# Groups of two batches with 256-column q/k products in place of groups of four with 512

## The chip, the cores and the metric

One core of one Trainium2 chip. The metric is the device time of one execution in microseconds (us).

## The reference, cut to what matters

Four graph layers over 128 batches of 128 nodes x 512 features, all in float32, each followed by a residual and a layer norm. The change touches only the last one, a masked multi-head attention:

```python
# layer 3, x: (128 batches, 128 nodes, 512), 8 heads of 64
qkv  = x @ w_qkv
attn = softmax(where(adj == 0, -inf, q @ k.T * 64**-0.5))
o    = (attn @ v) @ w_proj + b_proj
out  = o + layernorm(o) * gamma + beta
```

## The kernel before

Python chains (one per batch, some per group) ask a small planner, `Plan`, for their turn on an engine and for buffers. The planner holds its own estimate of every duration and fixes one static order of all instructions. So a change of group size or of a buffer count changes two things: the instructions of q and k, and the order of everything.

```python
G = 4                                   # batches that share one xT and the q/k products
BUFS = {"tr": 3, "mm": 3, "sc": 1, ..., "xT": 1, "v": 8, "qkT": 2, ...}

class Plan:
    def at(self, r):                    # earliest start of a request, by the planner's clock
        engine, _, take, _, _ = r["want"]
        t = max(r["ready"] + (MARGIN if engine == "PE" else 0.0), self.free.get(engine, 0.0))
        return max([t, *(self.slots[name][self.next[name]] for name in take())])
    def run(self):                      # the earliest request next; ties: urgent, then rank
        while self.requests:
            t, _, _, n = min((self.at(r), r["want"][4], r["rank"], n)
                             for n, r in enumerate(self.requests))
            ...                         # cut

def query_key(gr, c):                   # one of 8 chains of a group: 128 rows of q or k
    yield gr.turned                     # all G batches are turned into xT
    yield w3_in
    ...                                 # cut: ask for PE, a PSUM bank, and once for qkT
    p = product(lambda k: wqkv_sb[:, k, c * P : (c + 1) * P], lambda k: gr.xT[:, k, :])
    gr.read("xT", G + 2 * K)            # xT is free after the group's q, k and v products
    ...                                 # cut: copy to qkT, ACT for q, DVE for k

# per batch: mixed (L203) -> product (L195) -> ... -> turn into xT (L534) -> values ->
#   scores (L553, 64-row tiles) -> softmax -> two DMAs turn the probabilities ->
#   probabilities times v (L600, 64-column tiles) -> projection (L195) -> norm -> store
```

The last four batches are started 16 ranks early.

## Time and profile before

| | |
|---|---|
| time | 3414.68 us, median of 3 (3414.14 to 3414.78) |
| TensorE busy | 3378.9 of 3412.8 us |
| records of 512 columns for q and k | 2048 |
| TensorE waits shown | 24 us in 3412.8 |

The lines of the page for the q/k products and for the two copies out of PSUM. The columns are: line, engine, operation, output and inputs, shapes, count, then busy us, mean ns of one record, then idle time of the engine before them with what ended it. PE is TensorE, PEld its weight loads, DVE VectorE, ACT ScalarE and POOL GpSimd.

```profile
L195 PE MATMUL mm<-xT,wqkv_sb 128*128 128x512 f32 x2048 | 898.7, 594 | 5.2 <-DVE x L481 2.9 <-DVE qkT L442 1.5 <-ACT xT L536 0.8
L442 DVE COPY qkT<-mm 128x512 f32<-128x512 f32 x128 | 87.3, 682 | 247.4 <-PE mm L195 247.2
L440 ACT ACTIVATE qkT<-mm 128x512 f32<-128x512 f32 x128 | 75.4, 589 | 383.0 <-PE mm L195 383.0
```

The mean of 594 ns is the length of one record from start to end. Records overlap, so the cost of one is the distance between two starts, 429 ns. The copies have 247 and 383 us of idle time ahead of them: they wait for TensorE, never the reverse for long.

The end of the run, from TensorE's timeline (start, length, group, idle before it with what ended it):

```profile
3359.63 1.16 PE L553 MATMUL sc<-qkT 64*128 64x128 f32 x16
...
3373.80 1.16 PE L553 MATMUL sc<-qkT 64*128 64x128 f32 x16
3378.09 1.98 PE L600 MATMUL tr<-prT,v 128*64 128x128 f32 x16 [3.13 <-DMA prT<-p_d]
3381.73 5.17 PE L195 MATMUL mm<-wproj_sb,oT 128*128 128x512 f32 x8 [1.67 <-ACT oT L609]
...
3399.54 3.70 PE L195 MATMUL mm<-wproj_sb,oT 128*128 128x512 f32 x8 [0.74 <-ACT oT L609]
```

After its last scores TensorE has nothing to do until the first probabilities arrive (3.13 us). The wait costs twice: the next two chains take 1.98 and 5.17 us where the same chains take 1.09 and 3.70 elsewhere. The busy time by stretch shows a granted clock of 0.76 from 3380 to 3390 us.

### The profile page before, as it was taken

The page shows a single profiled execution, that of the slowest core. Times are in us where ns is not written, and L with a number is a line of the kernel's source. Part 1 is how long each engine was busy: PE and PEld are TensorE (multiplying, and loading weights), DVE is VectorE, ACT ScalarE, POOL GpSimd, SP SyncE. Part 2 cuts the span into 40 slices and gives each one's busy share as a digit, 9 for nine tenths or more (in the row PEclk, how much of TensorE's full clock was granted, in tenths as well). Part 3 has the DMA queues.
Part 4 walks back from the last instruction along what each step waited for, and adds up shares of the span by engine and source line. Part 5 has one row for each costly group of instructions (what it writes and reads, how often), then busy time and mean ns, then how long its engine had stood idle before and what let it go on. Part 6 is the DMA issues. An engine that isn't in the chain of part 4 may idle for free.

```text
span 3412.8 us, 39442 instructions
## 1 busy us (share of the span) xinstructions
PE 3378.9 (99%) x13193; PEld 1727.3 (51%) x13193; DVE 2588.1 (76%) x5399; ACT 1251.9 (37%) x3585; POOL 981.2 (29%) x1031
## 2 busy tenths in 40 slices
PE   9999999999999999999999999999999999999998
PEld 5555555545455455455555555555555545555543
DVE  7776976788777787777877777877778777797766
ACT  3433343334334233342343333433324334244332
POOL 2222422223221333223332223322233222341222
PEclk9999999999999999999999999999999999999999
DMA  4022121202121122111222112221112211121112
GB/s 155 32 86 71 54 75 56 87 30 78 67 77 53 47 78 78 62 60 46 79 76 68 62 48 71 78 68 65 56 56 78 77 60 59 50 78 59 53 69 79
DMA packets 169354, 228.58 MB, mean 67 GB/s; under 512 B 43456, under 2 KB 117312, under 8 KB 169152
## 3 DMA queue, kind: packets, MB, share of 16 engines
q1 hardware_dynamic: 169152, 226.08, 19.5%
q8 instruction: 104, 1.70, 0.2%
q14 instruction: 98, 0.80, 0.1%
HBM read 116.98 MB, written 109.05 MB: 66 GB/s over the span
## 4 chain that ended last, share of the span: by engine, by line
PE 92%; DVE 7%; issue 1%; DMA 0%; ACT 0%; POOL 0%; SPq 0%; POOLq 0%; DVEq 0%; ACTq 0%
PE mm L195 73%; PE tr L203 6%; PE sc L553 4%; PE tr L600 4%; PE mm L515 3%; PE tr L534 2%; DVE st L161 1%; DVE scr L488 1%; DVE x L182 0%; DVE x L507 0%; DVE mv L163 0%; DVE x L481 0%; PE tr L380 0%; DVE x L506 0%; DVE ve L165 0%
## 5 line engine op out<-in xcount | busy, mean ns | idle before, releaser
L195 PE MATMUL mm<-w_sb,yT 128*128 128x512 f32 x2048 | 921.0, 595 | 0.5 <-ACT yT L206 0.5
L195 PE MATMUL mm<-xT,wqkv_sb 128*128 128x512 f32 x2048 | 898.7, 594 | 5.2 <-DVE x L481 2.9
L168 POOL TENSOR_TENSOR rstd<-ve,neghalf 128x1 f32<-128x1 f32 x640 | 446.4, 698 | 1268.5 <-DVE ve L165 1103.3
L195 PEld LDWEIGHTS mm<-xT,wqkv_sb 128*128 128x128 f32 x2048 | 384.7, 190 | 468.5 <-issue 447.0
L195 PEld LDWEIGHTS mm<-w_sb,yT 128*128 128x128 f32 x2048 | 375.5, 190 | 410.4 <-issue 398.1
L195 PE MATMUL mm<-wqkv_sb,xT 128*128 128x512 f32 x1024 | 467.2, 599 | 0.0
L195 PE MATMUL mm<-wproj_sb,oT 128*128 128x512 f32 x1024 | 458.1, 596 | 3.8 <-ACT oT L609 3.8
L188 POOL TENSOR_TENSOR x<-x,beta_sb 128x512 f32<-128x512 f32 x128 | 186.0, 1463 | 937.4 <-PE tr L534 937.4
L571 ACT ACTIVATE pr<-pr,nmx 128x128 f32<-128x128 f32 x1024 | 398.8, 394 | 137.3 <-DVE nmx L567 137.2
L161 DVE BATCH_NORM_STATS2 st<-x 128x6 f32<-128x512 f32 x512 | 349.9, 683 | 4.7 <-ACT x L522 3.4
L177 ACT ACTIVATE x<-x,nmr,rstd 128x512 f32<-128x512 f32 x256 | 206.0, 810 | 288.1 <-DVE nmr L175 284.2
L195 PEld LDWEIGHTS mm<-wproj_sb,oT 128*128 128x128 f32 x1024 | 191.8, 191 | 234.5 <-issue 227.6
L560 DVE TENSOR_TENSOR pr<-sc,maskb 128x1024 f32<-128x1024 f32 x128 | 156.6, 1224 | 191.0 <-PE sc L553 185.3
L195 PEld LDWEIGHTS mm<-wqkv_sb,xT 128*128 128x128 f32 x1024 | 187.0, 190 | 208.7 <-issue 200.6
L442 DVE COPY qkT<-mm 128x512 f32<-128x512 f32 x128 | 87.3, 682 | 247.4 <-PE mm L195 247.2
L206 ACT COPY yT<-tr 128x512 f32<-128x512 f32 x256 | 148.3, 584 | 292.6 <-PE tr L203 290.8
L188 POOL TENSOR_TENSOR x<-x,o 128x512 f32<-128x512 f32 x128 | 180.2, 1408 | 153.6 <-DVE o L617 153.1
L440 ACT ACTIVATE qkT<-mm 128x512 f32<-128x512 f32 x128 | 75.4, 589 | 383.0 <-PE mm L195 383.0
L488 DVE SCALAR_TENSOR_TENSOR scr<-x,wa_rows 128x512 f32<-128x512 f32 x256 | 200.5, 783 | 9.4 <-ACT x L177 3.0
L188 POOL TENSOR_TENSOR x<-x,bias_sb 128x512 f32<-128x512 f32 x128 | 176.7, 1387 | 67.8 <-PE tr L203 57.1
L571 ACT ACTIVATION_READ_ACCUMULATOR pr<-pr,nmx 128x1 f32 x1024 | 195.3, 191 | 0.0
L609 ACT COPY oT<-tr 128x512 f32<-128x512 f32 x128 | 75.0, 586 | 273.4 <-PE tr L600 273.2
(65 smaller groups left out, 3753.6 us busy)
## 6 DMA issues: line engine op xcount, KB each, us to landing
p_d<-pt SPq DMA_DIRECT2D x128, 512.0 KB, 2.6
prT<-p_d SPq DMA_DIRECT2D x128, 512.0 KB, 3.7
x<-in_x SPq DMA_DIRECT2D x128, 256.0 KB, 2.6
out<-x SPq DMA_DIRECT2D x128, 256.0 KB, 2.0
e_d<-et SPq DMA_DIRECT2D x64, 128.0 KB, 1.7
eT<-e_d SPq DMA_DIRECT2D x64, 128.0 KB, 2.2
wqkv_sb<-in_L_gnn_w_qkv SPq DMA_DIRECT2D x1, 3072.0 KB, 10.8
w_sb<-in_L_gnn_weight SPq DMA_DIRECT2D x1, 1024.0 KB, 5.7
```

The source lines that it names most:

```text
L161: nc.vector.bn_stats(st, src)
L168: nc.gpsimd.tensor_tensor(rstd, ve, neghalf, op=ALU.pow)
L177: nc.scalar.activation(xb, xb, AF.Identity, bias=nmr, scale=rstd)
L188: nc.gpsimd.tensor_tensor(dst, dst, other, op=ALU.add)
L195: nc.tensor.matmul(p, lhs(k), rhs(k), start=(k == 0), stop=(k == K - 1))
L203: nc.tensor.matmul(p[:, k, :], xb[:, k * P : (k + 1) * P], nodes, start=True, stop=True)
L206: nc.scalar.copy(yT, p)
L488: nc.vector.scalar_tensor_tensor(scr, xb, 1.0, wa_rows[:, j, :], op0=ALU.mult, op1=ALU.mult, accum_out=gr.s[:, b, j : j + 1],)
L553: nc.tensor.matmul(sc[:, j, c, :], gr.qkT[rws, c, nodes], gr.qkT[rws, K + c, nodes], start=True, stop=True,)
L560: nc.vector.tensor_tensor(pr, sc.rearrange("p j c m -> p (j c) m"), maskb[:, None, :].to_broadcast([P, H, P]), op=ALU.add,)
L571: nc.scalar.activation(pr[:, j, :], pr[:, j, :], AF.Exp, bias=nmx[:, j : j + 1], accum_out=sums[:, j : j + 1],)
L600: nc.tensor.matmul(p[j * HD : (j + 1) * HD, c, :], valued.v[:, (2 * c + j) * HD : (2 * c + j + 1) * HD], prT[:, j * K + c], start=True, st ...
```

## The change

The intent: smaller groups let q, k and the scores of a pair start without waiting for four batches, and more buffers let the next pair be turned while the last is still read. The PSUM tile of a product stays 512 columns wide, so that two blocks of q or k rows of a pair (2 x 256) share one tile and one copy.

```diff
-G = 4
+G = 2
-    ... "xT": 1, "v": 8, "qkT": 2,
+    ... "xT": 2, "v": 8, "qkT": 3,
-            self.turned, self.qk = Event(G), Event(2 * K)
+            self.turned, self.qk = Event(G), Event(K)
-            for n in range(2 * K):
-                plan.start(query_key(groups[g], n // 2 + K * (n % 2)), g * G + n / (2 * K) - ...)
+            for n in range(K):
+                plan.start(query_key(groups[g], n // 2 * 2 + K * (n % 2)), g * G + n / K - ...)
@@ query_key
-        p = product(lambda k: wqkv_sb[:, k, c * P : (c + 1) * P], lambda k: gr.xT[:, k, :])
-        gr.read("xT", G + 2 * K)
+        p = bank([P, 2, G * P], "mm")
+        for j in range(2):
+            for k in range(K):
+                nc.tensor.matmul(
+                    p[:, j, :], wqkv_sb[:, k, (c + j) * P : (c + j + 1) * P], gr.xT[:, k, :],
+                    start=(k == 0), stop=(k == K - 1),
+                )
+        gr.read("xT", G + K)
# cut: the copies write qkT[:, c : c + 2, :]; the load order is kept as it was for groups of four
```

More of the change, by code (lines that the diff above doesn't have):

```diff
@@ L30 @@
     "tr": 3, "mm": 3, "sc": 1,
-    "x": 16, "yT": 3, "e": 2, "et": 1, "eT": 2, "ex": 2, "xT": 1, "v": 8, "qkT": 2,
+    "x": 16, "yT": 3, "e": 2, "et": 1, "eT": 2, "ex": 2, "xT": 2, "v": 8, "qkT": 3,
     "pr": 2, "pt": 1, "prT": 2, "oT": 2, "o": 2,
@@ L273, in loads @@
         landing(bias0_in, P)
-        for i in range(2, G):
+        for i in range(2, 4):
             yield from load(i)
@@ L281, in loads @@
         plan.start(logit_rows(a_sb, slot), 0)
-        for i in range(G, 2 * G):
+        for i in range(4, 8):
             yield from load(i)
@@ L289, in loads @@
         landing(scalars_in, 2 * P)
-        for i in range(2 * G, 3 * G):
+        for i in range(8, 12):
             yield from load(i)
@@ L297, in loads @@
         landing(w3_in, (4 * K + 3) * P)
-        for i in range(3 * G, NB):
+        for i in range(12, NB):
             yield from load(i)
@@ L367, in group @@
                 plan.start(attention1(groups[g], h), g * G + 2 * h - (16 if g * G >= NB - 4 else 0))
-            for n in range(2 * K):
-                plan.start(query_key(groups[g], n // 2 + K * (n % 2)), g * G + n / (2 * K) - (16 if g * G >= NB - 4 else 0))
+            for n in range(K):
+                plan.start(query_key(groups[g], n // 2 * 2 + K * (n % 2)), g * G + n / K - (16 if g * G >= NB - 4 else 0))
         return groups[g]
@@ L435, in query_key @@
             bp = got
-        p = product(lambda k: wqkv_sb[:, k, c * P : (c + 1) * P], lambda k: gr.xT[:, k, :])
-        gr.read("xT", G + 2 * K)
+        p = bank([P, 2, G * P], "mm")
[6 more added lines that the diff above has]
+        gr.read("xT", G + K)
         yield use("ACT" if c < K else "DVE", 0.69, urgent=True)
+        dst = gr.qkT[:, c : c + 2, :]
         if c < K:
-            nc.scalar.mul(gr.qkT[:, c, :], p, HD**-0.5)
+            nc.scalar.mul(dst, p, HD**-0.5)
         else:
             nc.vector.tensor_copy(
-                gr.qkT[:, c, :].rearrange("p (b c r) -> p b c r", b=G, c=Q),
-                p.rearrange("p (b r c) -> p b c r", b=G, c=Q),
+                dst.rearrange("p j (b c r) -> p (j b) c r", b=G, c=Q),
+                p.rearrange("p j (b r c) -> p (j b) c r", b=G, c=Q),
             )
@@ L459, in values @@
         give(bp)
-        gr.read("xT", G + 2 * K)
+        gr.read("xT", G + K)
         event.slot = bv
```

## The prediction

> **What bounds the kernel now.** I read the page first (busy shares, slices, chain that ended last), then the TensorE instruction groups with their shapes, then the timeline of TensorE in the middle and at both ends, then TensorE's waits, then busy time per stretch.
>
> From the page:
>
> ```profile
> PE 3378.9 (99%) x13193; PEld 1727.3 (51%) x13193; DVE 2588.1 (76%) x5399; ACT 1251.9 (37%) x3585; POOL 981.2 (29%) x1031
> PEclk9999999999999999999999999999999999999999
> PE 92%; DVE 7%; issue 1%; DMA 0%; ACT 0%; POOL 0%; SPq 0%; POOLq 0%; DVEq 0%; ACTq 0%
> ```
>
> TensorE is busy for 3378.9 of 3412.8 us, at full granted clock, and is 92% of the chain that ended last. Only 33.9 us is idle. But a busy PE need not be at its peak, so I need the time from one matmul start to the next. The timeline of TensorE, middle of the run (start, length, instructions), gives it:
>
> ```profile
> 2002.18 13.90 PE L195 MATMUL mm<-xT,wqkv_sb 128*128 128x512 f32 x32
> 2015.91 0.38 PE L380 MATMUL tr<-ident,s 128*128 128x128 f32 x2
> ...
> 2031.05 3.70 PE L195 MATMUL mm<-wqkv_sb,xT 128*128 128x512 f32 x8
> 2034.68 1.16 PE L553 MATMUL sc<-qkT 64*128 64x128 f32 x16
> 2035.77 3.70 PE L195 MATMUL mm<-wqkv_sb,xT 128*128 128x512 f32 x8
> ...
> 2095.43 2.84 PE L203 MATMUL tr<-adjT,x 128*128 128x128 f32 x24
> ```
>
> Each float32 product shows as two MATMUL records (a 4-step chain is x8); a transpose as one. Thirty-two records of 512 columns start at 2002.18 and what follows starts at 2015.91: 13.73/32 = **429 ns** each, across four chain ends with no gap. Twenty-four of 128 columns take 2098.10 - 2095.43 = 2.67 (the next record starts at 2098.10): **111.3 ns** each. Two numbers thus fix the cost of a record by its width.
>
> Does that account for the whole? Records of 512 columns: 2048 + 2048 + 1024 + 1024 + 256 = 6400, times 0.429 = 2746 us. Full-array records of 128 columns: 2697 x 0.1113 = 300 us. A score chain (x16) takes 1.09 us to the next start, and the 8-record chain after it 3.63 where 8 x 0.429 is 3.43, so 1.29 x 128 = 165 us. The chains on prT and v take about 1.03 plus two losses of 0.1 around them: 1.23 x 128 = 157 us. Sum 3368, against 3379 busy. So the kernel is a sum of matmuls at their steady pitch, plus mode changes; the bound is **the amount of TensorE work**, not its waits.
>
> The waits of TensorE, whole run (us in total, times, longest), show what a better order could still win:
>
> ```profile
> PE mm L195 <- ACT oT L609: 3.8, 4, 1.7
> PE tr L600 <- DMA prT<-p_d: 3.1, 1, 3.1
> PE mm L195 <- DVE x L481: 2.9, 1, 2.9
> PE tr L203 <- DMA x<-in_x: 2.8, 2, 1.5
> PE tr L305 <- DMA adj_sb<-in_adj: 2.8, 1, 2.8
> PE mm L515 <- DVE qkT L442: 2.7, 1, 2.7
> PE mm L195 <- DVE qkT L442: 1.5, 1, 1.5
> ```
>
> By stretch: about 7.7 us idle in the first 60 us (start-up loads; PE is busy 14.41, 18.76 and 19.13 of three times 20 us), 8.5 us between 400 and 1600 us (397.58 of 400 and 793.85 of 800), nothing from 1600 to 3300, and in the last 53 us 16.9 + 7.7 + 8.5 + 3.2 = 36.3 busy, so some 16.6 us idle. Of these about 9.5 us follow the last product (it starts at 3399.54 and ends at 3403.24): the last batch's normalisation and store.
>
> **What the Trainium skill says.** "TensorE: Matmul & The Clock Gate", section "Back-to-back issue gap", gives N/2.4 ns + 2.5 ns for a warm, isolated matmul. A float32 record here seems to take two array cycles a column: 512 x 2/2.4 + 2.5 = 429.2, and the trace's 429 agrees. For 128 it gives 109.2, the trace has 111.3, so the fixed part is 2.5 to 5 ns. The same page, section "Step-by-step: what each phase is for", says that the next weights load while this matmul runs; the trace agrees, as loads of 190 ns (mean) vanish under a 429 ns pitch and even under 111 ns (eight loads in 0.97 us). "TensorEngine Tiling (Array Packing)", section "Key Properties", says that changing tiling mode drains TensorE; the 0.1 to 0.2 us lost beside each 64-row or 64-column chain agrees. "PSUM — Partial Sum Buffer", section "The four PSUM rules", forbids two open accumulation groups in one bank; the new code closes the first half's before it opens the second's, so it is legal and needs no wait.
>
> **The change, part by part.**
>
> 1. **Twice as many q/k records, half as wide.** Before: 32 groups x 8 chains x 8 records = 2048 of 512 columns. After: 64 groups x 4 double chains x 2 x 8 = 4096 of 256. Columns in all are unchanged, the weights for q and k are loaded twice as often. Pitch at 256: a straight line through 111.3 (128) and 429 (512) gives 111.3 + 128 x 317.7/384 = 217.2 ns; the skill's form gives 256 x 2/2.4 + 2.5 = 215.8. Two of them cost 434.4 or 431.6 in place of 429: +2.6 to +5.4 ns for each of the 2048 old records, **+5 to +11 us**, all on the path, because TensorE is the bound. I take +8.
> 2. **Weight loads.** 2048 more, at 190 ns and pulled ahead. At a pitch of about 216 they stay covered: the 128-column chains already sustain one every 111 ns. Cost 0.
> 3. **Accumulation.** The same 256 columns are added to again after 216 ns. The `mixed` chains accumulate two records on the same 128 columns at 111 ns pitch with no loss. Cost 0.
> 4. **Copies out of PSUM.** 64 x 4 = 256 copies of 512 columns, as before 32 x 8: ACT 589 ns and DVE 682 ns each. The innermost runs (32) and element counts stay. Cost 0, and hidden anyway: DVE has 24% spare, ACT 63%.
> 5. **Buffers.** xT goes from one buffer of four batches to two of two: equal bytes, but the next pair may be turned while the previous one is still read. qkT goes from two of four to three of two: 24 KB a partition in place of 32. This removes waits only where TensorE waits, and that is nowhere from 1600 to 3300 us. The 7.1 us under L481 and L442 are mid-run and could go or move: I take -3.
> 6. **Tail.** Before, the last group computes all eight q/k chains (64 records, 27 us) and only then its scores; DVE is busy only 7.53 of 20 us there, from 3340 to 3360. The last scores end near 3374.9 and the program 38 us later, with about 19 us of products left. After, the first pair's softmax runs beside the second pair's q/k products; the last pair then has one round of softmax and transfers (first score end to first use: 3360.7 to 3378.1, 17.4 us), less product work to fill it (some 9 us plus leftovers of the first pair), and the same 15 us from its last prT chain to the end. I estimate T + 33 in place of T + 38, with T up to a few us later: between -7 and +5, I take -3.
> 7. **Start.** Unchanged: bound by loads and by the adjacency, before any q/k chain (the first starts at 108 us).
>
> Sum: 3414.7 + 8 - 3 - 3, about **3417 us**.
>
> **The rivals.**
>
> (a) *A narrower matmul costs more than the line says*, for instance because a 190 ns load no longer hides under a 216 ns record when chains switch. If the pitch were 232, 4096 x 15 = +61 us, near 3478. For: the loads come almost back to back. Against: the 111 ns pitch with the same loads.
>
> (b) *The order gets worse.* The static plan is recomputed with other ranks and granularity; a pair of batches gives TensorE less independent work ahead, and DVE (76% overall, 38 of 40 us in 60 to 100) could become the local bound. For: q/k now arrive every 27 us in 14 us blocks, and each waits for only two turns. Against: 16 batches are in flight and other chains fill gaps; no wait on PE in the second half. Worth +5 to +40 us.
>
> (c) *The order gets better.* Bubbles (8.5 us) and the avoidable tail (about 7 us) go entirely: 3414.7 + 8 - 15, near 3407. The gain cannot be larger: 33.9 us is all the idle time there is, and some 17 us of that is loads and the last batch's own chain.
>
> (d) *Mode changes move.* Their count stays at 128 score and 128 prT chains, but which neighbour they have may change; at 0.1 us each, up to 10 us either way.
>
> **Range and chances.** The sure part is +5 to +11 us; tail and bubbles span about -15 to +15 around it, and (b) stretches the upper side. I choose 3403 to 3437. A gain of 2% is 68 us, twice the whole idle time: 0.01. A loss of 68 us needs (a) or a bad (b): 0.02. Within 2%: 0.97.
>
> **What would show each step right or wrong.** In the profile after: 4096 records `mm<-xT,wqkv_sb` of 128x256; in the timeline 64 of them from start to next start in 13.8 to 13.9 us (step 1); if it is 14.5 or more, (a) holds. Their mean length should be 592 - 256/1.2, about 379 ns. TensorE busy should rise to about 3384 to 3390 and its waits stay under 40 us; waits on DVE of tens of us mean (b). The 400 to 1600 stretch shows step 5, the last 53 us step 6. Copies at 589 and 682 ns confirm step 4. I am wrong if the pitch is off the line, or if the new order idles TensorE.

## The result

The changed kernel takes **3410.36 us** (median of 4, 3409.27 to 3411.25) against 3414.73 us before (median of 4, 3414.14 to 3417.1). The ratio is 0.9986, 95% interval 0.9968 to 1.0003. The ranges don't overlap, but the interval just touches 1: within 2%, and 4.4 us shorter by the medians.

From the page of the changed kernel, the busy line and the groups that answer to those of before:

```profile
PE 3379.5 (99%) x15241; PEld 2119.6 (62%) x15241; DVE 2593.1 (76%) x5399; ACT 1264.8 (37%) x3585; POOL 947.0 (28%) x1031
L439 PE MATMUL mm<-xT,wqkv_sb 128*128 128x256 f32 x4096 | 911.8, 380 | 0.0
L449 DVE COPY qkT<-mm 128x512 f32<-128x512 f32 x128 | 87.9, 687 | 150.5 <-PE mm L439 149.8
L447 ACT ACTIVATE qkT<-mm 128x512 f32<-128x512 f32 x128 | 76.3, 596 | 278.3 <-PE mm L439 278.0
```

There are twice the records, 380 ns long (379 was expected), and the same copies. TensorE is busy 3379.5 us, 0.6 more than before, though the narrower records alone should add 5. So something else on TensorE got shorter. Its timeline in the middle of the run:

```profile
2010.40 10.52 PE L439 MATMUL mm<-xT,wqkv_sb 128*128 128x256 f32 x48
2020.76 0.60 PE L541 MATMUL tr<-ident,x 128*128 128x128 f32 x4
...
2053.16 1.09 PE L607 MATMUL tr<-prT,v 128*64 128x128 f32 x16
2054.19 1.16 PE L560 MATMUL sc<-qkT 64*128 64x128 f32 x16
2055.28 3.70 PE L195 MATMUL mm<-w_sb,yT 128*128 128x512 f32 x8
```

The first two lines give the pitch: (2020.76 - 2010.40)/48 = 215.8 ns. The last three show what is new in the order: a probabilities chain and a score chain, both on 64-wide tiles, stand **next to each other**. Counted over the whole program, that happens at 28 places; in the kernel before at one.

The waits of TensorE (us in total, times, longest) and the end of its timeline:

```profile
PE tr L380 <- DVE scr L495: 6.4, 6, 2.0
PE tr L607 <- DMA prT<-p_d: 4.1, 3, 3.1
...
PE mm L195 <- ACT oT L616: 1.5, 2, 0.7
```

```profile
3369.60 1.16 PE L560 MATMUL sc<-qkT 64*128 64x128 f32 x16
3370.69 3.70 PE L195 MATMUL mm<-wqkv_sb,xT 128*128 128x512 f32 x8
...
3385.55 1.30 PE L607 MATMUL tr<-prT,v 128*64 128x128 f32 x16 [3.08 <-DMA prT<-p_d]
3387.59 6.44 PE L195 MATMUL mm<-wproj_sb,oT 128*128 128x512 f32 x8 [0.73 <-ACT oT L616]
3394.47 1.09 PE L607 MATMUL tr<-prT,v 128*64 128x128 f32 x16 [0.45 <-DMA prT<-p_d]
3396.31 3.70 PE L195 MATMUL mm<-wproj_sb,oT 128*128 128x512 f32 x8 [0.74 <-ACT oT L616]
```

The waits on the q/k copies are gone, others on DVE came. After the last scores three batches are left to finish in place of four, and after the wait for prT two in place of four. The wait of 3 us and the slow chain after it (6.44 us) are still there. "TensorE: Matmul & The Clock Gate" of the Trainium skill, section "HAM oscillation — how this bites in real kernels", warns of idle gaps of TensorE above some 3.4 us. In these traces shorter gaps were followed by a lower clock: after those of 3.08 and 3.13 us the granted clock was 0.50 for some 6.8 us. Two gaps in the middle (2.05 us, ending at 2862.8, in the changed kernel; 2.91 us, ending at 1260.5, before) were followed by 0.50 for some 3.4 us, while two others (2.05 us at 1437.8; 2.68 us at 857.4) were not. The account below counts what these stretches cost as loss, about 4.4 us before and 4.9 in the changed kernel.

**An account of TensorE.** For every record I took the time to the next record's start and split it: steady pitch (429.05 ns for 512 columns, 215.8 for 256, 111.3 for 128, and half of that, as a convention, for a 64-wide record), idle time that the profile shows, and the rest, which I call loss. The first 2.7 us, before TensorE's first record, are left out. The three add up to the start of the last record; then some 10 us follow.

| us | steady pitch | loss | idle | sum |
|---|---|---|---|---|
| before | 3273.6 | 104.9 | 21.4 | 3399.9 |
| changed | 3278.8 | 100.3 | 17.6 | 3396.7 |
| difference | +5.2 | -4.6 | -3.8 | -3.2 |

And the loss sits at a few kinds of places, each of them almost constant. Between 60 and 3300 us of the kernel before, the means are: 93 ns at the last full-width record ahead of a 64-wide chain; 146 to 147 ns at the end of a 64-wide chain; 91 to 102 ns in the first records after it. A score or a probabilities chain alone thus costs about 0.34 us besides its own work. Where two of different kind stand together, one entry (93) and one aftermath (104, the median) fall away, **0.197 us**. Where two probabilities chains stand together, a lone one's 147 ns end shrinks to 47 as well and the second runs 51 ns shorter, about 0.35 us (the last two from the run e14 below). For the change: 27 more places x 0.197 = 5.3 us, and the loss fell by 4.6.

So the theory is: the narrow records cost 5 us, the new order saves about as much at mode changes of TensorE (from full-width to 64-wide chains and back), and waits fall by 4 us, most of it at the end.

### The profile page after: what moved, and what is told of

Same layout as the page of the kernel before. It is cut to its first block, busy times and chain, and to the rows that moved or that the text cites. A ratio compares the mean times of both kernels' runs of the same rounds, so it can differ in the third digit from the quotient of the medians.

```text
span 3409.4 us, 43497 instructions
## 1 busy us (share of the span) xinstructions
PE 3379.5 (99%) x15241; PEld 2119.6 (62%) x15241; DVE 2593.1 (76%) x5399; ACT 1264.8 (37%) x3585; POOL 947.0 (28%) x1031
## 4 chain that ended last, share of the span: by engine, by line
PE 89%; DVE 9%; DMA 1%; issue 1%; ACT 0%; POOL 0%; SPq 0%; POOLq 0%; DVEq 0%; ACTq 0%
PE mm L195 46%; PE mm L439 25%; PE tr L203 5%; PE sc L560 4%; PE tr L607 4%; PE mm L522 3%; DVE st L161 2%; PE tr L541 2%; DVE scr L495 1%; DVE x L182 1%; DVE x L488 1%; DVE x L636 1%; DVE mv L163 0%; DVE t L633 0%; DVE ve L165 0%
## 5 line engine op out<-in xcount | busy, mean ns | idle before, releaser
L439 PE MATMUL mm<-xT,wqkv_sb 128*128 128x256 f32 x4096 | 911.8, 380 | 0.0
L439 PEld LDWEIGHTS mm<-xT,wqkv_sb 128*128 128x128 f32 x4096 | 771.1, 190 | 120.9 <-issue 14.3
L168 POOL TENSOR_TENSOR rstd<-ve,neghalf 128x1 f32<-128x1 f32 x640 | 422.3, 661 | 1518.1 <-DVE ve L165 1342.1
L188 POOL TENSOR_TENSOR x<-x,beta_sb 128x512 f32<-128x512 f32 x128 | 173.8, 1359 | 312.3 <-PE tr L541 312.0
L465 ACT COPY v<-mm 128x512 f32<-128x512 f32 x128 | 75.0, 586 | 387.6 <-PE mm L195 387.6
L188 POOL TENSOR_TENSOR x<-x,bias_sb 128x512 f32<-128x512 f32 x128 | 182.3, 1434 | 119.1 <-PE tr L203 107.4
```

The costliest lines, as they stand in the source:

```text
L168: nc.gpsimd.tensor_tensor(rstd, ve, neghalf, op=ALU.pow)
L188: nc.gpsimd.tensor_tensor(dst, dst, other, op=ALU.add)
L439: nc.tensor.matmul(p[:, j, :], wqkv_sb[:, k, (c + j) * P : (c + j + 1) * P], gr.xT[:, k, :], start=(k == 0), stop=(k == K - 1),)
```

## The experiments

Twelve kernels, all correct against the reference (there is no run e4 or e13). "Before" in each is measured on the same chip in the same rounds: 3415.0 to 3415.9 us. The changed kernel was not run again beside them, so differences to it are between rounds, and "before" moved by up to 1.2 us between those. The account of TensorE for all of them, worked out in the same way:

| run | time us | ratio to before (95%) | steady pitch | loss | idle | places with 64-wide neighbours |
|---|---|---|---|---|---|---|
| before | 3414.73 | | 3273.6 | 104.9 | 21.4 | 1 |
| changed | 3410.36 | 0.9986 (0.9968 to 1.0003) | 3278.8 | 100.3 | 17.6 | 28 |
| e1_halves | 3419.85 | 1.0014 (1.0001 to 1.0026) | 3278.8 | 105.8 | 20.5 | 1 |
| e2_quarters | 3448.14 | 1.0096 (1.0082 to 1.0109) | 3306.7 | 107.4 | 19.8 | 1 |
| e3_pairs_fewbufs | 3419.93 | 1.0014 (1.0001 to 1.0028) | 3278.8 | 97.1 | 28.3 | 32 |
| e5_hybrid2 | 3414.73 | 1.0000 (0.9987 to 1.0013) | 3273.8 | 105.8 | 22.2 | 2 |
| e6_paired_tiled | 3412.38 (its four fast runs) | 0.9992 (0.9978 to 1.0006) | | | | 88 |
| e7_paired_tiled_fours | 3415.66 | 1.0002 (0.9990 to 1.0015) | 3273.6 | 94.4 | 33.1 | 53 |
| e8_hybrid4 | 3422.51 | 1.0021 (1.0007 to 1.0035) | 3273.9 | 104.9 | 28.7 | 3 |
| e9_pairs_qk2 | 3410.83 | 0.9988 (0.9974 to 1.0002) | 3278.8 | 99.7 | 18.2 | 28 |
| e10_paired_early | 3409.43 | 0.9983 (0.9971 to 0.9996) | 3278.8 | 91.0 | 26.0 | 81 |
| e11_apart | 3428.49 | 1.0039 (1.0025 to 1.0052) | 3278.8 | 105.3 | 29.9 | 0 |
| e12_fours_xT2 | 3451.08 | 1.0104 (1.0090 to 1.0118) | 3273.6 | 114.1 | 50.1 | 11 |
| e14_paired_patient | 3379.36 | 0.9895 (0.9878 to 0.9911) | 3278.8 | 68.0 | 15.8 | 125 |

### The narrow records alone: e1 and e2

The kernel before, its groups, buffers and order untouched, with each q/k product cut in two (e1) or four (e2).

```diff
-        p = product(lambda k: wqkv_sb[:, k, c * P : (c + 1) * P], lambda k: gr.xT[:, k, :])
+        p = bank([P, D], "mm")
+        for part in range(2):                       # e2: 4, of 128 columns
+            cols = slice(part * 256, (part + 1) * 256)
+            for k in range(K):
+                nc.tensor.matmul(p[:, cols], wqkv_sb[:, k, c * P : (c + 1) * P], gr.xT[:, k, cols],
+                                 start=(k == 0), stop=(k == K - 1))
```

> The kernel before (groups of four, its order, its buffers), with each product for q and k made as two of 256 columns. Theory, pitch: 4096 records at 215.8 ns in place of 2048 at 429.0, +5.3 us on the path, all else the same (511 mode changes as before): about 3420 us, TensorE busy near 3384. Rival, narrower records are free because weight loads and records overlap: 3414 to 3415. Rival, loads that follow too closely: 3430 or more.

> As e1, but four products of 128 columns: 8192 records. Theory, pitch: 111.3 ns as in the other 128-column chains, 8192 x 0.1113 - 2048 x 0.429 = +33 us, about 3448; if the fixed part is only 2.5 ns as at 256 columns (109.2 ns), +16 us, 3431. Rival, free: 3415.

Measured: e1 3419.85 us, +4.7 by the medians; e2 3448.14 us, +33.0. From TensorE's timeline in the middle of e1 and then of e2:

```profile
2005.97 13.98 PE L440 MATMUL mm<-xT,wqkv_sb 128*128 128x256 f32 x64
2019.78 0.38 PE L380 MATMUL tr<-ident,s 128*128 128x128 f32 x2
```

```profile
2020.65 14.45 PE L440 MATMUL mm<-xT,wqkv_sb 128*128 128x128 f32 x128
2034.94 0.38 PE L380 MATMUL tr<-ident,s 128*128 128x128 f32 x2
```

The same work takes 13.81 us as 64 records and 14.29 as 128; as 32 of 512 columns it took 13.73. The pitches are 215.8 and 111.6 ns. Loss and idle stay within 3 us of before. Weight loads stay hidden in both, as the pitches show. Twice as many records cost 5 us; four times as many cost 33, because a record of 128 columns takes 3.7 ns more than half of one of 256, which in turn takes 1.3 ns more than half of one of 512. Rival (a) of the prediction is out.

### The buffers: e3 and e9

```diff
 # e3: the changed kernel with           # e9: the changed kernel with
-    "xT": 2, "qkT": 3                   -    "qkT": 3
+    "xT": 1, "qkT": 2                   +    "qkT": 2
```

> The changed kernel without the added buffers: one xT of two batches, two qkT. Theory, the buffers only remove a few bubbles: +0 to +6 us against the changed kernel, 3410 to 3416, since its order has 480 mode changes of TensorE against 484. Rival, the buffers carry the result (turns wait for the previous pair's q, k and values): idle of TensorE up by 15 us or more, 3425 or above.

> The changed kernel with two qkT buffers in place of three (xT stays at two). The planner makes the same order of instructions on every engine. Theory, the third qkT buffer is worth nothing: within 1.5 us of the changed kernel, 3409 to 3412. Rival, on the chip a copy out of PSUM waits for the buffer: 3414 or more.

e9 took 3410.83 us: the planner makes the same order on all engines, and the time stayed. The third qkT buffer is worth nothing. Building e3's program with three qkT gave the same order as e3 too, so e3's effect belongs to xT. e3 took 3419.93 us, 9.6 more than the changed kernel, against my own theory. Its mode changes fell as counted; its idle time rose by 10.7 us, 7.4 of them at the end of the run:

```profile
3346.03 3.60 PE L195 MATMUL mm<-wqkv_sb,xT 128*128 128x512 f32 x8
3349.46 1.04 PE L541 MATMUL tr<-ident,x 128*128 128x128 f32 x8
3351.28 10.63 PE L439 MATMUL mm<-xT,wqkv_sb 128*128 128x256 f32 x48 [0.78 <-ACT xT L543]
...
3376.22 1.16 PE L560 MATMUL sc<-qkT 64*128 64x128 f32 x16
...
3394.10 1.98 PE L607 MATMUL tr<-prT,v 128*64 128x128 f32 x16 [9.65 <-DMA prT<-p_d]
```

With one xT buffer the last pair is turned (L541, 3349.46) only after the values product of the pair ahead (3346.03) has let go of xT. So its last scores come 7 us later than in the changed kernel (3376.22 against 3369.60), less other work is left to cover the softmax and the two transfers, and TensorE waits 9.65 us in place of 3.08. **The second xT buffer is what makes pairs usable at the end of the run.**

### The end of the run without the buffer: e5 and e8

Groups of four, with only the last group (e5) or the last two groups (e8) as pairs, and one xT.

```diff
+    WIDE = NB // G - 1                              # e8: - 2
-        g, b = divmod(i, G)
+        g, b = divmod(i, G) if i < WIDE * G else (WIDE + (i - WIDE * G) // 2, i % 2)
 # cut: each group carries its size; q/k as in the changed kernel where it is 2
```

> The kernel before, but its last group of four is two pairs (256 columns for those two alone); buffers of before. Theory, the gain of the change comes partly from the tail: idle in the last 53 us down by 2 to 5 us, 3410 to 3413. Rival, the gain comes from the order in the middle (fewer mode changes, 484 against 511 before; here 510): within 1 us of before, 3414 to 3415.

> Groups of four, but the last eight batches in pairs, so that the batches that really finish last (120 to 123, as the last four are started early) are pairs too, which the first hybrid missed. Theory, tail: idle before the last product down by 2 us or more, 3411 to 3413. Rival, pairs alone do nothing for the tail, since they need the second xT buffer to be turned early: 3414 to 3420.

e5 was a miss of mine: since the last four batches start early, its pairs are not the batches that finish last, and its end is that of before (3414.73 us). e8 puts pairs there, and took 3422.51 us, 7.5 **more** than before: TensorE waits 10.77 us for the first prT of its last pair, after that pair too was turned only when the values ahead were done. Smaller groups alone make the end worse.

### The second xT buffer in groups of four: e12

```diff
-    "xT": 1, "v": 8
+    "xT": 2, "v": 5          # v cut to make room; with xT at 1 this leaves TensorE's order as before
```

> The kernel before, groups of four and full 512 columns, with two xT buffers in place of one; v goes from eight buffers to five to make room. 11 places with 64-wide neighbours (before: 1). Theory, the second xT buffer is what helps the end of the run, with groups of four too: turns of the group that finishes last come before the values of the group ahead, idle before the last product down by 2 us or more, and 10 x 0.17 = 1.7 us of neighbours: 3409 to 3412. Rival, it needs the pairs: 3414 or more.

3451.08 us, +36. The loss and the idle time rose throughout: the order bunches up, and transposes wait for DVE (17.3 us in 8 waits of L534 on L182). Why was not tested; that a buffer of four batches more lets the planner run ahead in larger steps is a guess. v also shrank. Worked out from the kernels without a run, the planner makes the same order on every engine with v at eight, so that the new order comes from xT; how much of the +36 us it explains on the chip was not measured. The run does not support the buffer without the pairs.

### The neighbours: e11, e6, e7, e10

If 28 places are worth 5 us, taking them away must cost 5 us. e11 is the changed kernel with a tie-break that avoids putting a 64-wide chain next to another; no such place was left. e6, e7 and e10 have the opposite rule.

```diff
+    def later(self, r):                             # tie-break among requests ready at once
+        if not r["want"][5] or not self.pairing:    # [5]: a 64-wide chain
+            return 1
+        if self.tiled:                              # the last TensorE chain was 64-wide
+            return 0                                # e11: 2
+        return 2 if self.free.get("PE", 0.0) - r["ready"] < 4.0 else 1      # e7: 8.0; e11: 0.0
-                (self.at(r), r["want"][4], ...
+                (self.at(r) - (0.5 if self.pairing and self.tiled and r["want"][5] else 0.0),  # e11: + 0.5
+                 self.later(r), r["want"][4], ...
+                self.pairing = self.now < 3200.0    # e10 alone; e6, e7, e11: always on
 # cut: the flag tiled is passed along with the request
```

> The changed kernel with the opposite rule: a 64-wide chain is never put next to another. No such place in place of 28. Theory, these 28 places are what the order of the pairs gained in the middle: +28 x 0.17 = +4.8 us, about 3415, more if waits are added. Rival, they are worth nothing: 3410 to 3411.

> The changed kernel with one rule added to its planner: the two kinds of 64-wide chains (scores, and probabilities times v) are put next to each other where both are ready, a lone one waits up to 4 us for a partner. Mode changes of TensorE fall from 484 to 405. Theory, each change costs about 0.18 us (86.9 us over 485 of them before, 82.3 over 461 after, between 60 and 3300 us): -79 x 0.18 = -14 us, about 3396, less what new waits take back. Rival, the fewer mode changes of the changed kernel were not where its gain came from: 3408 to 3412 with unchanged waits.

> The kernel before (groups of four) with the same rule, waiting up to 8 us: 415 mode changes in place of 511. Theory: -96 x 0.18 = -17 us, about 3397 to 3398, with no part of the change in it. Rival: 3413 to 3416.

> The changed kernel with the neighbour rule (wait up to 4 us for a partner) only while the planner's clock is below 3200 us, since in e7 the rule idled TensorE at the end (16.9 us against 7.8). 81 places where two 64-wide chains stand next to each other, 28 in the changed kernel. Theory, each such place saves one exit and one entry, about 0.17 us (e7: 52 places, 7.7 us): -53 x 0.17 = -9 us, 3401 to 3403, if the tail stays as in the changed kernel. Rival, the gain goes into new waits again: 3408 to 3415.

e11: 3428.49 us. The loss went back up from 100.3 to 105.3, +5.0, which is what the 28 places were said to be worth. But the time rose by 18, because idle rose by 12.3 us; most of that is one wait at the end (14.38 us for prT, after a score chain that came as late as 3383.93). An order rule cannot be changed in one respect alone.

e6: its profiled execution fell into a strange state (8173.48 us), told below, so there is no account of it. Its four fast executions lie between 3409.93 and 3414.63 us. The expected 3396 was missed.

e7, without any part of the change: loss 10.5 us lower, and not 17 as expected. Its places, 42 of them between two probabilities chains, should save some 16 us by the constants above. Between 60 and 3300 us the loss fell by 13.9; at the end it rose by 3.5, where waits of up to 5.1 us came with a granted clock of 0.50 (for 17 us from 3370.8 on). And idle rose by 11.7 us, 9.1 of them at the end. Net nothing, 3415.66 us.

e10, with the rule off at the end: the end is that of the changed kernel again (idle 4.6 us there), the loss is 9.3 us lower, and 9.1 us of new waits in the middle take it back (score chains that wait briefly for DVE, 6.4 us in 21 waits; prT). 3409.43 us, about 1 us below the changed kernel and not told apart from it.

So the loss follows the neighbours in e7, e10 and e11, and in e7 and e10 about as much comes back as waits, since the rule makes TensorE take a chain before its data is due.

### A version that beats both: e14

The same rule, but patient: a lone 64-wide chain lets any other ready TensorE work go first for up to 55 us, until a partner is ready. As long as it has other work, TensorE idles for the partner by at most 0.3 us of the planner's clock. 55, and the end of the rule at 3150 us, were picked from some hundreds of settings by the planner's own account (its estimated end, and the number of places), not on the chip.

```diff
-        return 2 if self.free.get("PE", 0.0) - r["ready"] < 4.0 else 1
+        return 2 if self.free.get("PE", 0.0) - r["ready"] < 55.0 else 1
-        self.at(r) - (0.5 if ...
+        self.at(r) - (0.3 if ...
-                self.pairing = self.now < 3200.0
+                self.pairing = self.now < 3150.0
```

> The changed kernel with the neighbour rule, now patient: a lone 64-wide chain lets any other ready TensorE work go first for up to 55 us, until a partner is ready; off in the last part of the run, as in e10. 125 places with 64-wide neighbours, 28 in the changed kernel. Theory, 0.17 us a place (e10: -9.3 us of overhead for 53 more places, but 8.4 us of new waits): -97 x 0.17 = -16 us, and few new waits, since TensorE never waits for the partner while it has other work: 3392 to 3398. Rival, what neighbours save comes back as waits again, as in e10: 3405 or more.

Measured: **3379.36 us** (3378.82 to 3381.27), ratio to before 0.9895. That is more than expected. From its timeline in the middle:

```profile
2020.10 1.95 PE L215 MATMUL tr<-adjT,x 128*128 128x128 f32 x16
2021.98 1.97 PE L619 MATMUL tr<-prT,v 128*64 128x128 f32 x32
2023.88 1.16 PE L572 MATMUL sc<-qkT 64*128 64x128 f32 x16
2024.97 3.72 PE L451 MATMUL mm<-xT,wqkv_sb 128*128 128x256 f32 x16
```

Three 64-wide chains stand together: two of probabilities as one run of 32 records (1.90 us to the next start, where two alone take 2 x 1.03), and the scores right after. There are 125 such places, 46 of them between two probabilities chains. By the constants above, 51 more mixed places x 0.197 and 46 x 0.35 make 26 us; the loss fell by 32.3 against the changed kernel, 26.5 of it between 60 and 3300 us. Some 4.5 us more come from the end, where the order happened to leave no wait above 0.74 us, so that no chain there ran slowly. Idle is 15.8 us against 17.6, though new waits did come (score chains for DVE, 8.7 us in 11 waits). I had expected 16 us, since I counted every place at 0.17. Not tested: the same patience in groups of four. So e14 does not show that it needs the pairs.

## Why the prediction was right or wrong

The time, 3410.4, lies in the range of 3403 to 3437 and 6.6 us below the centre. The centre had the sign wrong: 2 us slower was expected, and it is 4 us faster. The bound was named rightly: in every run with an account but e12 the time is TensorE's pitch and loss, plus 16 to 33 us of idle and some 15 us before its first and after its last record start.

1. **Narrow records: right, a little too dear.** The range was +5 to +11 us with +8 taken. The trace gives +5.2 and e1 +4.7. The skill's form (215.8) held to the digit; the straight line through 128 columns (217.2) was the wrong choice, since a record of 128 columns (111.3) is longer than that form gives (109.2). The forecast for TensorE's busy time, 3384 to 3390 us, failed: it was 3379.5, because loss fell.
2. **Weight loads: right.** 4096 loads hide, and 8192 in e2.
3. **Accumulation: right.** No loss appears in chains of 256 or 128 columns.
4. **Copies: right.** 596 and 687 ns against 589 and 682.
5. **Buffers: the size was about right, the reason incomplete.** I took -3 for waits in the middle; between 60 and 3300 us idle fell by 1.2 (8.6 to 7.4). The worth of the second xT, 9.6 us in e3, sits mostly at the end, where I had not looked for it. The third qkT is worth nothing (e9).
6. **Tail: the sum was right by luck, the mechanism was not.** I took -3 and had the program end 33 us after the last scores in place of 38, with these scores no earlier. They ended 4.2 us earlier (3370.8 against 3375.0), and the end came 38.7 us after them (37.8 before). Idle at the end did fall by 2.8 (7.8 to 5.0). I credited the pairs. Pairs without the second buffer leave more idle time there than before (12.4 us in e3, 14.2 in e8), because the last pair is turned late.
7. **Start: right**, though the first q/k chain now starts at 95 us and not at 108.

Missing from the sum is what I had put down as rival (d): the neighbours of the mode changes, -4.6 us. I said up to 10 us either way and counted zero, so that the total came near by luck: this gain made up for the dearer records. Rival (c), a better order, is thus what happened in kind, through mode changes and waits alike. But its bound, that the gain cannot be larger than the idle time, was wrong: in e14 idle is only 5.6 us below before, and loss 36.9. Both that bound and the 10 us of (d) took for fixed what a busy TensorE loses at mode changes. Rival (b) did not happen here; e11 and e12 show how easily it does.

The account: +5.2 - 4.6 - 3.8 = -3.2 us in the profiled executions, -4.4 in the medians. What is left open: how much of the 4.6 us is due to the pairs and how much to the planner's chance. e3, with pairs and another order, has 32 such places, which speaks for the pairs; groups of four in another order have 11 (e12), so the order alone can make some.

## What to carry to other kernels

When an engine is 99% busy, measure from start to start and look for what is not work: here 105 us of loss, some 87 of it at mode changes between full and 64-wide chains (some 255 chains x 0.34), were five times all that TensorE idled (21.4 us). Grouping such chains pays only where the waits that it brings are smaller than the saving, so let other ready work go first. And judge a static order by its end: in e3, e7, e8 and e11 most of the added idle time fell after 3300 us.

## What the Trainium skill lacked or had wrong

- "TensorEngine Tiling (Array Packing)", section "Key Properties", says that changing the mode drains TensorE, without a figure. The runs show 93 ns at the last full record, 147 ns at the end of the 64-wide chain and about 104 ns after it, 0.34 us for a lone chain. They also show that going from 64-column to 64-row chains costs 147 ns but neither entry nor aftermath.
- "TensorE: Matmul & The Clock Gate", section "Back-to-back issue gap": the form N/2.4 + 2.5 ns, with two cycles a column for float32 records, agrees within 0.2 ns at 512 and 256 columns (429.05 and 215.8 ns), and 2 to 2.5 ns short at 128 (111.3 to 111.6). The sustained 81 and 131 ns that the section gives for pairs of load and matmul do not describe these float32 records.
- No page says how a float32 matmul shows in a trace: as two such records, and a float32 transpose as one. The counts do (a chain of four products is x8, four transposes are x4).
- "Perfetto Trace Analysis", section "Identifying the Most-Contended Engine", advises MFU (the share of peak FLOP/s) and the busy share of LDWEIGHTS in place of that of the matmuls. The LDWEIGHTS share rose here from 51% to 62% while the time fell by 0.1%, only because the loads doubled for one layer. That share alone would have misled; the distance between starts did not.
- The same TensorE page, section "HAM oscillation — how this bites in real kernels", speaks of idle gaps above about 3.4 us as what slows the clock. Here gaps of 3.08 and 3.13 us were followed by chains of 6.44 and 5.17 us in place of 3.70, and even gaps of 2.05 and 2.91 us by 3.4 us at a granted clock of 0.50, though not each time.
- No page describes an execution like one of e6, which took 8173.48 us while four others took 3409.93 to 3414.63. Eight records of 512 columns took 9.5 us there (at 4018 us) and later 7.4 us (at 6017 us) in place of 3.43, while DVE's busy time stayed at 2582.8 us. Its page has no row for the clock, so its trace seems to hold no clock record, and the mean of 1.000 listed for it should not be read as a measurement. The cause is open.
